# Four-layer image network: the values of the first four units of layer 0 are projected in turns -1 to 2, and the keys' norms are spread at another place

## The chip, the cores and the metric

The kernel runs on one core of a Trainium2 chip. The metric is the device time of one execution in microseconds (us), taken as the median over several runs. An execution covers both images of the batch and all four layers. TensorE does the matrix products (PE in the profile, with its weight loads shown as PEld), VectorE (DVE) and ScalarE (ACT) do most element-wise work, GpSimd (POOL) some of it, and the queue of SyncE (SP) issues the transfers.

## The reference

The input is two images of 512 channels and 64 x 64 pixels in float32. Four residual layers follow each other; each one normalizes its input by groups of channels (16 channels share a mean and a variance), computes something and adds it to its input. The change touches layer 0 alone, so only that is shown, shortened:

```python
q = xf @ W_q + b_q                      # 8 heads of 64 channels, 4096 tokens
q_norm = q / |q|;  q_scaled = (q_norm + query_embedding) * softplus(temperature)
k_l, v_l = xf @ W_kv + b_kv             # k_l is divided by its norm, per head
attn_local = q_scaled . k_l at the 3 x 3 neighbours of each token      # 9 numbers
xs = layernorm(mean over 4 x 4 of gelu(xf @ W_sr + b_sr))              # 256 pooled tokens
k_pool, v_pool = xs @ W_kv + b_kv
attn = softmax(concat(attn_local, q_scaled @ normalized(k_pool)))
lt = q_norm @ learnable_tokens + learnable_bias + attn[:9]
out = (sum over the 9 neighbours of lt * v_l + attn[9:] @ v_pool) @ W_proj + b_proj
```

Layers 1 to 3 (a deformable attention, a mixture of max-pools, and an attention by random features) are the same before and after.

## The kernel before, in words

**Layout.** An image lies in SBUF as four blocks of 128 channels by 4096 tokens. One block of channels is two heads. Layer 0 works on *units*: a unit is one block of channels times 1024 tokens (16 rows of the image), so there are 4 units to a block (`UN`) and 16 in all, taken block after block. Products are made in *blocks* of 512 tokens, one PSUM bank each. A float32 product of 128 x 128 by 512 shows as two instructions, so the projection of one block of tokens (four products over the input channels, line 134, `project`) is eight instructions. Five banks named `mm` serve everything (`bank`), besides one for the sums of the taps and one for a copy of the queries.

**The run of layer 0** (`Local.run`). First the pooled tokens: 32 projections with the gelu. Then a loop over *turns* i = -4 to 16. In turn i the keys of unit i+4 are projected, the queries of unit i+3, and the products of queries with the nine shifted keys (the *taps*) are made for unit i+1; unit i attends to the pooled tokens, and unit i-1 weighs its values by the nine taps. Each of these stages is a Python generator; `in_turn` advances all of them by one step after another, and so ten *rounds* make a turn. The order in which the generators write instructions is the program order. Within a round it is: norms, tap products, attention, weighing, tap sums, projections, spread of the norms (`normed`). A planner (a list scheduler with its own cost model) then orders each engine's instructions by program order as far as it believes them ready. In turns with the flag `steady`, PE alone is excepted: it keeps the program order (`manual_schedule` for PE). Before, `steady` holds in turns 3 to 11.

**Values.** Values are projected by `value`: eight instructions on PE, and an ACTIVATE on ACT (line 2364) that adds the bias and writes the block into the framed image `vx`. When a unit is the last of its block of channels, the next block's weights are fetched by a transfer on SP's queue (`fetch`). In turns 3 and later the values of unit i+1 are made; the values of the first four units are made earlier, unit 0 in turn -4, units 1 and 2 in turn -3, unit 3 in turn -2. Turns -4 to -2 also hold the computation of the pooled keys and values (`pooled_heads`, a chain of small steps over all engines), of which turn -4 has the first twelve steps.

**Norms.** `norms` (round 1 and 2 of a turn) takes the squares of the turn before: products on PE that sum them by heads (line 2303), then on DVE a transpose, an inverse square root by integer shift and three Newton steps, and a transpose back into `sq` (lines 2306 to 2318). `normed` spreads the results over the 64 channels of each head by a small product on PE (line 2330, two for keys and two for queries) and multiplies keys or queries by them on DVE (line 2338). Keys go into the framed image `kx`, queries stay. `learned` then makes the products with the learnable tokens and the scaled queries. In a steady turn the keys' spread stands at the end of round 3, the queries' at the end of round 4, `learned` in round 6; in other turns in rounds 5, 6 and 7.

**Attention and weighing.** `attend` takes four pairs of products with the pooled keys (line 2433, `exponentials`), each followed by exponentials on ACT (line 2437), two groups of products with the pooled values (line 2443, `values(0)` and `values(1)`), and the sum of the exponentials (lines 2459 and 2462). `weigh` reads the spread tap weights back by transfers, copies them into banks on ACT (line 2526), and multiplies them with `vx` on DVE (line 2534); POOL adds (line 2539). In steady turns tap products are made in pairs (five instructions of DVE on line 2381 instead of nine), the third pair is queued behind the last multiplication of the keys, and two half sums of POOL (line 2452) go to `sq`.

Of the kernel before, what the change touches and what calls it, by code (L numbers as in the profile page):

```python
# [12 lines left out]
ALU = mybir.AluOpType  # L13
# [3 lines left out]
P = 128  # L17
C = 512
KC = C // P
W = 64  # L20
# [1720 lines left out]
class Queries:  # L1741
# [29 lines left out]
    def run(self, Y, dst, fp, pp, ppo, ppd, load):  # L1771

        nc, ratio = self.nc, fp.tile([P, NH], F32, name="ksum_ratio")
        self.Y = Y
        nc.vector.reciprocal(ratio, self.ksum[:, 0, :])
        nc.vector.tensor_tensor(ratio, ratio, self.ksum[:, 1, :], ALU.mult)
        in_turn(self.score(0, fp, pp), self.prepare(1, pp))
        for blk in range(NB):
            stages = [self.attend(blk, ratio, dst, fp, pp, ppo, ppd)]
            if 1 <= blk < NB - 1:  # L1780
                stages.append(self.prepare(blk + 1, pp))
            if blk + 1 < NB:
                stages.append(chain([None], self.score(blk + 1, fp, pp)))
            if load and 0 <= blk - 3 < KC:
                stages.append(load(blk - 3))
            if load and 0 <= blk - 4 < KC:
                st = fp.tile([P, NB, 6], F32, name="gn_st0")
                stages.append(self.statistics(Y, st, blk - 4, pp))
            in_turn(*stages)
        big = LIMIT * math.exp(-LIMIT)  # L1790
        nc.vector.reciprocal(self.low, self.low)
        for t in (self.low, self.high):
            nc.vector.tensor_scalar(t, t, big, None, ALU.mult)
            self.net.at_most(t)
# [143 lines left out]
class Local:  # L1938
# [77 lines left out]
    def run(self):  # L2016


        self.nmean = self.net.stats[:, 0]
        xs = self.pooled_tokens()  # L2020
        heads = self.pooled_heads(xs)
        units = KC * self.UN
        unit = lambda u: u if 0 <= u < units else None
        self.pending = []
        for i in "qkv":
            self.fetch(i, 0)
        for i in range(-4, units + 1):
            k, q, ahead, u, before = (unit(i + n) for n in (4, 3, 1, 0, -1))
            self.steady = self.UN <= i + 1 and i < units - 4
            streams, ended = [], []  # L2030
            stages = [self.norms(streams, ended)]
            if ahead is not None:
                stages.append(self.tap_products(ahead))
            if u is not None:
                stages.append(self.attend(u))
            if before is not None:
                stages.append(self.weigh(before))
            if ahead is not None:
                stages.append(self.tap_sums(ahead))
            values = ([ahead] if i >= self.UN - 1 and ahead is not None  # L2040
                      else {-4: [0], -3: [1, 2], -2: [3]}.get(i, []))
            stages.append(self.projections(k, q, values, streams))
            stages.append(self.normed(ended))
            if i < -2:
                stages.append(islice(heads, 12 if i == -4 else None))
            if i == units - 3:
                stages.append(self.fetch_output())
            if i > units - 3:
                stages.append(self.output(i - units + 2))
            if self.steady:  # L2050
                with self.net.tc.manual_schedule(engines={mybir.EngineType.PE}):
                    in_turn(*stages)
            else:
                in_turn(*stages)

        self.nc.sync.dma_start(self.next_w, self.d["w_q1"].rearrange("(kc p) o -> p kc o", p=P))
        in_turn(self.output(KC - 1))
# [263 lines left out]

    def normed(self, ended):

        nc = self.nc
        for _ in range(3 if self.steady else 5):
            yield
        for which in "kq":
            mine = [(e, self.bank()) for e in ended if e[2] == which]
            for (s, rows, *_), ps in mine:
                nc.tensor.matmul(ps, self.cst[32 * s:32 * s + 2, C_ROW:C_ROW + P], rows, start=True,  # L2330
                                 stop=True)
            for (_, _, _, u, j, part, _), ps in mine:
                out = part
                if which == "k":
                    y = 1 + u % self.UN * self.UY + j * self.UY // 2
                    out = self.kx[:, y:y + self.UY // 2, 1:W + 1]
                    part, ps = (a.rearrange("p (y x) -> p y x", x=W) for a in (part, ps))
                self.multiplied = nc.vector.tensor_tensor(out, part, ps, ALU.mult).ins  # L2338
            yield
        if self.steady:  # L2340
            yield
        if mine:
            self.learned(mine[-1][0][3])
        yield

    def learned(self, u):

# [69 lines left out]
        self.el[u] = el  # L2417
        yield

    def attend(self, u):  # L2420

        nc = self.nc
        cc = u // self.UN
        qs, el = self.qs[u % 3], self.el[u]
        out = self.att()
        prob, half = {}, {}
        self.out[u] = out
        heads = [slice(h * HD, (h + 1) * HD) for h in range(2)]

        def exponentials(j, k2):  # L2430
            pS = [self.bank() for _ in range(2)]
            for h, c in enumerate(heads):
                nc.tensor.matmul(pS[h], self.kp[c, cc, k2 * P:(k2 + 1) * P],
                                 qs[c, j * TB:(j + 1) * TB], start=True, stop=True)
            prob[j, k2] = [self.prob() for _ in range(2)]
            for h in range(2):
                nc.scalar.activation(prob[j, k2][h], pS[h], AF.Exp)  # L2437

        def values(j):
            psO = self.bank()  # L2440
            for k2 in range(2):
                for h, c in enumerate(heads):
                    nc.tensor.matmul(psO[c, :], self.vp[:, k2, cc * P + h * HD:][:, :HD],
                                     prob[j, k2][h], start=(k2 == 0), stop=(k2 == 1))
            nc.scalar.copy(out[:, j * TB:(j + 1) * TB], psO)
            halved(j)

        def halved(j):
            if j not in half:
                half[j] = self.halves if not j else self.sq[2:] if self.steady else prob[1, 1]  # L2450
                for h in range(2):
                    nc.gpsimd.tensor_tensor(half[j][h], prob[j, 0][h], prob[j, 1][h], ALU.add)  # L2452

        def sums():
            psD = self.bank()
            blocks = [slice(j * HD, (j + 1) * HD) for j in range(2)]
            for h in range(2):
                for j, b in enumerate(blocks):
                    nc.tensor.matmul(psD[b, :], self.cst[:, C_EVEN + h:C_EVEN + h + HD],
                                     half[j][h], start=(h == 0), stop=False)  # L2460
            for b in blocks:
                nc.tensor.matmul(psD[b, :], self.cst[b, C_SD:C_SD + HD], el[b, :], start=False,
                                 stop=True)
            return psD

        exponentials(0, 0)
        yield
        exponentials(0, 1)
        yield
        if self.steady:  # L2470
            yield
        values(0)
        if not self.steady:
            yield
        exponentials(1, 0)
        yield
        exponentials(1, 1)
        if self.steady:
            halved(1)
        yield  # L2480
        values(1)
        yield
        if not self.steady:
            yield
        psD = sums()

        nc.vector.transpose(psD, psD)
        two = psD.rearrange("p (b n r) -> p b n r", n=16, r=2)[:, :, 0]
        nc.vector.reciprocal(two, two)
        nc.vector.transpose(self.recip.rearrange("p (b n r) -> p b n r", n=16, r=2),  # L2490
                            bcast(two, 2, 16))
        yield
        el = self.el.pop(u)
        nc.vector.tensor_tensor(el, el, self.recip, ALU.mult)
        nc.vector.tensor_tensor(el, el, self.lt.pop(u), ALU.add)
        if self.steady:
            yield
        self.spread = self.rows()
        for j in range(2):
            nc.sync.dma_start(self.spread[:, j * TB:(j + 1) * TB], el[j * HD:(j + 1) * HD, :])  # L2500
        self.fetch_tap(u, 0)
        yield
        self.fetch_tap(u, 1)
        yield
# [231 lines left out]
```

## Time and profile before

| | us |
|---|---|
| runs | 5098.28, 5098.58, 5102.41 |
| median | 5098.58 |
| the profiled execution, its own time | 5100.09 |
| its span, first to last instruction | 5098.3 |
| PE busy in the span | 4835.1 |
| DVE busy | 3067.0 |
| ACT busy | 1817.9 |
| POOL busy | 1843.8 |
| mean granted clock of TensorE | 0.981 |

A turn is best found in the trace by its products on line 2303, of which each turn from -3 on has one group. Counted from there, the turns of the first image begin at 194.16 (turn -3), 230.32 (-2), 253.49 (-1), 285.79 (0), 321.51 (1), 365.32 (2), 411.09 (3), 456.53 (4) and then every 42.54 us. Those of the second image begin at 2726.34, 2760.81, 2785.67, 2817.97, 2853.69, 2897.95, 2943.87 and 2989.63 us. The stretch before turn -3, with turn -4, begins at 153.67 us in the first image and at 2684.60 in the second, where the first products of values are seen.

In a table of stretches each row gives its bounds and its length, for every engine the busy time and the number of instructions, then the granted clock of TensorE (1.00 is full speed), and the transfers' share and rate. In a timeline each row gives start, duration, engine, line, operation, names, shapes and count, and in brackets the idle time of the engine ahead of it and what ended that. Profile names are those of the buffers that the tiles lie in: `vx`, `kx`, keys and queries show as `big`, most small tiles of the layer as `late`.

### The profile page before, as it was taken

How to read it: one execution, taken by the hardware profiler on the slowest of the kernel's cores; microseconds unless marked ns; L12 is line 12 of the kernel's file. 1: busy time of each engine (PE TensorE's matmuls, PEld its weight loads, DVE VectorE, ACT ScalarE, POOL GpSimd, SP SyncE). 2: the span in 40 equal slices, each digit the busy share in tenths (PEclk: the TensorE clock that was granted, in tenths of full speed). 3: DMA queues.
4: the chain of work that ended last, by engine and by line, in shares of the span. 5: the costliest groups of instructions: out<-in, count | busy, mean ns of one | idle time of the engine just before them, and what ended most of it. 6: DMA issues, size and time to landing. Idle time of an engine off the chain costs nothing. (4 is left out here: it accounts for less than half of the span.)

```text
span 5098.3 us, 48031 instructions
## 1 busy us (share of the span) xinstructions
PE 4835.1 (95%) x17027; PEld 1992.3 (39%) x17027; DVE 3067.0 (60%) x4014; ACT 1817.9 (36%) x3479; POOL 1843.8 (36%) x1214
## 2 busy tenths in 40 slices
PE   7999999899999999999999999998999999999998
PEld 3423332555334444433344233335543344444333
DVE  4266777644679533477732677776446794334766
ACT  1245555334323233322112555552343232333221
POOL 0035666500320045454500456654013201454554
PEclk9999999999999999999999999999999999999999
DMA  3035556600000000211110355565000000000111
GB/s 151 3 80 141 149 147 172 169 23 10 1 1 17 2 1 1 67 58 46 56 72 3 95 141 149 147 181 149 19 10 1 17 1 1 1 1 23 38 46 45
DMA packets 124748, 309.82 MB, mean 61 GB/s; under 512 B 20882, under 2 KB 33682, under 8 KB 122964
## 3 DMA queue, kind: packets, MB, share of 16 engines
q1 hardware_dynamic: 124500, 306.68, 20.7%
q8 instruction: 136, 2.23, 0.2%
q14 instruction: 112, 0.92, 0.1%
HBM read 258.11 MB, written 48.50 MB: 60 GB/s over the span
## 5 line engine op out<-in xcount | busy, mean ns | idle before, releaser
L134 PE MATMUL mm<-big,w 128*128 128x512 f32 x2496 | 1178.8, 616 | 33.0 <-DVE big L2338 9.5
L134 PEld LDWEIGHTS mm<-big,w 128*128 128x128 f32 x2496 | 458.0, 193 | 717.8 <-issue 560.1
L2539 POOL TENSOR_TENSOR late<-late,big 128x1024 f32<-128x1024 f32 x192 | 455.4, 2372 | 235.6 <-DVE big L2534 203.5
L2381 DVE TENSOR_TENSOR prods<-qs,big 128x1024 f32<-128x1024 f32 (+1 forms) x216 | 335.3, 1569 | 66.4 <-PE tap L2408 56.2
L1639 POOL TENSOR_TENSOR big<-big 128x512 f32<-128x512 f32 x224 | 277.9, 1274 | 219.3 <-ACT big L1630 219.3
L2534 DVE TENSOR_TENSOR big<-big,mm 128x512 f32<-128x512 f32 x384 | 252.0, 680 | 127.1 <-ACT mm L2526 126.8
L2526 ACT COPY mm<-big 128x512 f32<-128x512 f32 x428 | 245.2, 596 | 124.6 <-DMA big<-rows 80.9
L1630 ACT ACTIVATE big<-mm,ed 128x256 f32<-128x256 f32 x512 | 193.5, 489 | 233.0 <-DVE top L1626 200.4
L2452 POOL TENSOR_TENSOR late<-late 128x512 f32<-128x512 f32 x92 | 115.4, 1274 | 440.3 <-ACT late L2437 416.7
L2539 POOL TENSOR_TENSOR late<-late,tap 128x1024 f32<-128x1024 f32 x96 | 226.7, 2361 | 113.8 <-DVE tap L2534 100.7
L1442 POOL TENSOR_TENSOR wq<-prob 128x512 f32<-128x512 f32 x48 | 70.8, 1497 | 503.1 <-ACT prob L1439 503.1
L1894 PE MATMUL mm<-k,w 128*128 128x512 f32 x512 | 238.5, 609 | 12.5 <-DVE k L1887 7.5
L1626 DVE TENSOR_REDUCE top<-mm 128x1 f32<-128x512 f32 x256 | 158.9, 682 | 148.2 <-PE mm L1557 148.2
L1604 PE MATMUL mm<-w,big 128*128 128x512 f32 x512 | 236.6, 606 | 0.0
L134 PE MATMUL mm<-big,wq 128*128 128x512 f32 x512 | 232.2, 602 | 2.7 <-ACT off_t L1223 2.7
L1195 PE MATMUL mm<-big,wo 128*128 128x512 f32 x512 | 234.7, 604 | 0.0
L1352 PE MATMUL acc<-big,diag 128*128 128x512 f32 x512 | 226.9, 601 | 4.6 <-ACT diag L1357 4.6
L973 POOL TENSOR_TENSOR group_stats<-group_stats,cst 128x1 f32<-128x1 f32 (+1 forms) x20 | 12.1, 622 | 570.6 <-DVE group_stats L972 510.4
L1884 DVE RECIPROCAL psD<-psD 128x512 f32<-128x512 f32 x64 | 215.1, 3361 | 1.9
L134 PE MATMUL mm<-big,big 128*128 128x512 f32 x464 | 201.7, 594 | 0.5 <-DVE b_sr L1011 0.5
L2408 PE MATMUL tap<-prods,cst 128*32 128x512 f32 x1152 | 195.3, 604 | 5.1 <-DVE prods L2381 4.3
L1439 ACT ACTIVATE prob<-mm 128x512 f32<-128x512 f32 x256 | 133.0, 603 | 171.4 <-PE mm L1436 171.1
(404 smaller groups left out, 8154.3 us busy)
## 6 DMA issues: line engine op xcount, KB each, us to landing
big<-rows SPq DMA_DIRECT2D x428, 256.0 KB, 4.1
tap<-rows SPq DMA_DIRECT2D x212, 256.0 KB, 4.1
yd<-late SPq DMA_DIRECT2D x32, 512.0 KB, 3.1
lost_all<-lost SPq DMA_DIRECT2D x128, 128.0 KB, 3.0
out<-big SPq DMA_DIRECT2D x64, 256.0 KB, 2.0
big<-in_W_kv SPq DMA_DIRECT2D x8, 1024.0 KB, 8.7
rows<-late SPq DMA_DIRECT2D x64, 128.0 KB, 3.3
prods<-yd SPq DMA_DIRECT2D x16, 512.0 KB, 4.9
```

The source lines that it names most:

```text
L134: self.nc.tensor.matmul(ps, w[:, kc, :], X[:, kc, blk * TB:(blk + 1) * TB], start=(kc == 0), stop=(kc == KC - 1))
L1195: nc.tensor.matmul(ps, w[:, kc, oc * P:(oc + 1) * P], att[:, kc, :], start=(kc == 0), stop=(kc == KC - 1))
L1352: nc.tensor.matmul(accs[b], dg, src[:, b * TB:(b + 1) * TB], start=(j == 0), stop=(j == 6))
L1604: nc.tensor.matmul(ps, X[:, kc, lo:lo + P], wv[:, kc, :], start=(kc == 0), stop=(kc == KC - 1))
L1639: nc.gpsimd.tensor_tensor(a, a, part, ALU.add)
L1884: nc.vector.reciprocal(psD, psD)
L1894: nc.tensor.matmul(ps, self.wo[:, kc, oc * P:(oc + 1) * P], qs[:, kc, :], start=(kc == 0), stop=(kc == KC - 1))
L2381: self.nc.vector.tensor_tensor(self.pair(u, k)[:, :n].rearrange("p k (y x) -> p k y x", x=W), bcast(qs.rearrange("p (y x) -> p y x", x=W), ...
L2408: nc.tensor.matmul(ps[32 * q:32 * q + 32, :], self.cst[:, C_TAPW + 16 - 2 * k:][:, :32], self.pair(u, k)[:, 0, j * TB:(j + 1) * TB], start ...
L2526: nc.scalar.copy(ps, part)
L2534: nc.vector.tensor_tensor(part.rearrange("p (y x) -> p y x", x=W), self.vx[:, y:y + self.UY // 2, dx:dx + W], ps.rearrange("p (y x) -> p y ...
L2539: nc.gpsimd.tensor_tensor(out, out, t, ALU.add)
```

## The change

The values of unit i+1 are now made in turn i for every i from -1 on; turns -4 to -2 make none. The flag `steady`, with its fixed order on PE, its pairs of tap products and its places of steps, holds in turns 0 to 11. The spread of the keys' norms leaves `normed` in steady turns: it is now called by `attend`, in round 3, behind `values(0)` and ahead of `exponentials(1, 0)`. The spread of the queries' norms stays in round 4, `learned` in round 6.

```diff
         for i in range(-4, units + 1):
             k, q, ahead, u, before = (unit(i + n) for n in (4, 3, 1, 0, -1))
-            self.steady = self.UN <= i + 1 and i < units - 4
+            self.steady = 0 <= i < units - 4
...
             if u is not None:
-                stages.append(self.attend(u))
+                stages.append(self.attend(u, ended))
...
-            values = ([ahead] if i >= self.UN - 1 and ahead is not None
-                      else {-4: [0], -3: [1, 2], -2: [3]}.get(i, []))
+            values = [ahead] if ahead is not None else []
             stages.append(self.projections(k, q, values, streams))
...
     def normed(self, ended):
 
-        nc = self.nc
-        for _ in range(3 if self.steady else 5):
+        for _ in range(4 if self.steady else 5):
             yield
         for which in "kq":
-            mine = [(e, self.bank()) for e in ended if e[2] == which]
...
-            yield
+            if not self.steady or which == "q":
+                last = self.spread_norms(ended, which)
+            if not self.steady:
+                yield
         if self.steady:
             yield
-        if mine:
-            self.learned(mine[-1][0][3])
-        yield
+            yield
+        if last is not None:
+            self.learned(last)
+        yield
+
+    def spread_norms(self, ended, which):
+
+        nc = self.nc
+        mine = [(e, self.bank()) for e in ended if e[2] == which]
+        for (s, rows, *_), ps in mine:
+            nc.tensor.matmul(ps, self.cst[32 * s:32 * s + 2, C_ROW:C_ROW + P], rows, start=True,
+                             stop=True)
+        for (_, _, _, u, j, part, _), ps in mine:
+            out = part
+            if which == "k":
+                y = 1 + u % self.UN * self.UY + j * self.UY // 2
+                out = self.kx[:, y:y + self.UY // 2, 1:W + 1]
+                part, ps = (a.rearrange("p (y x) -> p y x", x=W) for a in (part, ps))
+            self.multiplied = nc.vector.tensor_tensor(out, part, ps, ALU.mult).ins
+        return mine[-1][0][3] if mine else None
...
         if self.steady:
             yield
         values(0)
+        if self.steady:
+            self.spread_norms(ended, "k")
         if not self.steady:
             yield
         exponentials(1, 0)
```

More of the change, by code (lines that the diff above doesn't have):

```diff
@@ L2322, in normed @@
     def normed(self, ended):
-        nc = self.nc
-        for _ in range(3 if self.steady else 5):
+        for _ in range(4 if self.steady else 5):
             yield
         for which in "kq":
-            mine = [(e, self.bank()) for e in ended if e[2] == which]
[L2329 to L2338, printed above, removed]
-            yield
+            if not self.steady or which == "q":
+                last = self.spread_norms(ended, which)
+            if not self.steady:
+                yield
         if self.steady:
             yield
-        if mine:
-            self.learned(mine[-1][0][3])
+            yield
+        if last is not None:
+            self.learned(last)
         yield
+    def spread_norms(self, ended, which):
[12 more added lines that the diff above has]
+        return mine[-1][0][3] if mine else None
     def learned(self, u):
@@ L2418, in tap_sums, with attend @@
         yield
-    def attend(self, u):
+    def attend(self, u, ended):
         nc = self.nc
```

## The prediction

> **What bounds the kernel now.** I read the page first, then a table of stretches over the turns of layer 0, the waits of PE, and the timelines of single turns.
>
> ```profile
> PE 4835.1 (95%) x17027; PEld 1992.3 (39%) x17027; DVE 3067.0 (60%) x4014; ACT 1817.9 (36%) x3479; POOL 1843.8 (36%) x1214
> ```
>
> PE is the bound: a step is worth what it adds to PE's work, its idle time, or its slow clock. The stretches of the first image (turn -4, -3, ... 4):
>
> ```profile
> 153.67:194.16 40.49, 39.38 (x130) 21.18 (x128) 6.42 (x11) 10.06 (x18) 0.71 (x1) 1.00 0.00 1
> 194.16:230.32 36.16, 35.20 (x93) 14.71 (x93) 7.83 (x26) 7.47 (x12) 3.39 (x3) 0.91 0.00 0
> 230.32:253.49 23.17, 22.13 (x66) 8.18 (x65) 11.20 (x23) 8.10 (x12) 0.00 (x0) 1.00 0.04 12
> 253.49:285.79 32.30, 29.65 (x98) 9.30 (x97) 16.34 (x28) 10.82 (x16) 0.00 (x0) 0.95 0.03 9
> 285.79:321.51 35.72, 35.72 (x149) 11.06 (x148) 20.22 (x33) 14.73 (x26) 5.01 (x4) 1.00 0.20 46
> 321.51:365.32 43.81, 40.81 (x149) 12.46 (x146) 32.84 (x55) 24.63 (x44) 26.15 (x13) 0.92 0.47 126
> 365.32:411.09 45.77, 41.80 (x132) 13.49 (x127) 28.91 (x49) 24.66 (x44) 26.08 (x13) 0.93 0.45 126
> 411.09:456.53 45.44, 42.96 (x153) 13.45 (x153) 33.24 (x51) 26.43 (x47) 26.18 (x13) 1.00 0.61 163
> 456.53:499.07 42.54, 41.84 (x153) 13.16 (x153) 32.02 (x49) 25.31 (x45) 26.17 (x13) 1.00 0.55 147
> ```
>
> The point is the rows of turns 1 and 2 (the fourth and third from the end) against the last one. Turns 1 and 2 project no values and yet take 43.81 and 45.77 us; turn 4, with values, takes 42.54. They lose 3.0 and 4.0 us idle and, at clocks of 0.92 and 0.93, 3.5 and 3.2 us of speed. A block of values costs PE 3.43 us (sixteen instructions of line 134 took 7.13, eight 3.70), a unit 6.9. Turn 0, never idle, needs 35.72; with 6.9 added that is turn 4's 42.6. So values in turns 0 to 2 fit, if those turns then run like turn 4.
>
> The lead-in's cover, first in turn -4 (second image), then turns -2 and -1 (first image):
>
> ```profile
> 2688.03 1.89 PE L2109 MATMUL mm<-late,cst 128*128 128x256 f32 x8
> 2689.76 3.60 PE L134 MATMUL mm<-big,w 128*128 128x512 f32 x8
> 2693.19 1.84 PE L2119 MATMUL mm<-cst,late 128*128 128x1 f32 x16
> 2696.12 0.71 PE L2128 MATMUL mm<-cst,ln_rs 128*128 128x128 f32 x4 [1.09 <-POOL ln_rs L2123]
> 2696.67 5.29 PE L134 MATMUL mm<-big,w 128*128 128x512 f32 x8
> ```
> ```profile
> 236.05 1.13 PE L2330 MATMUL mm<-sq,cst 2*128 2x512 f32 x4 [1.04 <-DVE sq L2318]
> ...
> 265.59 1.13 PE L2330 MATMUL mm<-sq,cst 2*128 2x512 f32 x4 [1.73 <-DVE sq L2318]
> ```
>
> The row at 2689.76 is a block of values standing between two links of the pooled chain; the row at 2696.67 is a block of keys that could have filled the 1.09 us ahead of line 2128 and did not. Last, the regular turn on PE, and its DVE one turn later (add 42.54):
>
> ```profile
> 506.00 1.94 PE L2443 MATMUL mm<-late,vp 128*64 128x512 f32 x8
> 507.86 1.13 PE L2433 MATMUL mm<-big,kp 64*128 64x512 f32 x4
> ...
> 509.92 1.13 PE L2330 MATMUL mm<-sq,cst 2*128 2x512 f32 x4
> ...
> 512.63 3.70 PE L134 MATMUL mm<-big,w 128*128 128x512 f32 x8 [0.53 <-DVE big L2338]
> ```
> ```profile
> 548.52 0.72 DVE L2318 STREAM_TRANSPOSE sq<-mm 128x512 f32<-128x512 f32 x1
> 553.84 1.28 DVE L2338 TENSOR_TENSOR big<-big,mm 128x512 f32<-128x512 f32 x2
> ```
>
> Keys are multiplied on DVE at 553.84 to 555.12, and the first block of keys' projection starts then (512.63 + 42.54 = 555.17) after 0.53 us idle: a bank is freed late. The waits of PE put that at 4.7 us for nine turns.
>
> **The change part by part** (for one image; both have the same turns).
>
> *Eight blocks of values leave turns -4 to -2.* 8 x 3.43 = 27.4 us of PE. Their eight evictions on ACT (0.69 us each) are off the path on either side: ACT is busy 8 to 10 us in those turns, 25 of 43 in turns 1 and 2. One transfer of weights (128 x 512 floats, 256 KB) moves on SP's queue from turn -2, where transfers have a share of 0.04, to turn 2, behind the taps' transfers (0.45). It is due at the start of turn 3, some 35 us later; in the regular turns the same transfer leaves no wait on PE. The framing of `vx` on POOL (0.28 and 0.21 us) loses a wait for an eviction.
>
> *The cover that goes.* Six waits of PE's chain stand open without values: last gelu to line 2109 2.7 us (154.1 to 156.83, ACT and three steps of DVE); 2109 to 2119 2.4 (a DVE and an ACT step, 159.46 to 161.77); 2128 to 2145 2.7 (two DVE steps, 166.46 to 169.09), if the keys that now stand there go into the first two; the pooled keys' roots 3.6 (DVE, then 2.90 of POOL, to 199.2); the last eviction of turn -3 1.4; and the norms of turn -2, 4.6 (231.51 to 236.00 on DVE). Sum 17.4. Nothing opens if the planner puts the next projections of keys and queries there, which are owed anyway; all 17.4 if it never does. Both are seen: the 1.09 above was not filled with the keys right behind it, while at 180.62 two instructions of line 2159 went into a wait of line 2152. I take the middle, 8.7.
>
> *Two blocks of values enter turn -1.* 6.9 us, of which its 2.65 us of idle time take the first part: +4.2.
>
> *Slow clock in the lead-in.* It costs 4.9 us now (0.09 x 36.16 + 0.05 x 32.30), in the second image 6.7. Fewer waits in turn -1 and more before speak against each other: 0. Bounds: -5 (none left) and +10 (each of the six waits brings one slow stretch of 3.4 us at half speed, 1.7).
> Here the Trainium skill ("TensorE: Matmul & The Clock Gate", "Why this matters for your kernels") says that waits under about 3 us leave the clock alone. The trace differs: the slow stretch in turn -1 follows a wait of 1.73 us, those of turns 1 and 2 waits of 2.46 and 2.40. By the rule only the waits of 3.6 and 4.6 us could slow it, at most +3.4 in place of +10.
>
> Lead-in: -27.4 + 8.7 + 4.2 + 0 = -14.5; from -28 (no cover lost, no slow clock) to +4 (all open).
>
> *Turns 0 to 3.* Now 35.72 + 43.81 + 45.77 + 45.44 = 170.7 (second image 171.7). After, four regular turns with the keys' spread moved, 4 x 42.01 (below), and half of what turn 3 paid for entering the fixed order (45.44 - 42.54 = 2.9), 1.5, as turn 0 has no weighing: 169.5. That is -1.2 and -2.2. Pairs of tap products save DVE 9 x 1.21 - (4 x 2.28 + 1.21) = 0.6 a turn, off the path. Bounds: -3.7, and +11 if each takes 45.4.
>
> *Keys' spread behind values(0).* No work is added. From line 2303 the regular turn has `values(0)` at +6.9, pooled products at +8.8, the spread at +10.85; DVE has the rows ready at +7.63. The spread goes to +8.8, 1.1 us after its rows, so PE should not wait; DVE is idle from +7.63 to +10.06, multiplies then, and the banks come free near +11.2, ahead of the keys' projection at +13.0. The 0.53 goes. Behind the spread on PE stand the pooled products, which move from +8.8 to +9.85, and their exponentials on ACT; `values(1)`, which needs them, starts at +18.2, so that is covered by 8 us. What is late next is the 0.17 us for an exponential, which stays. In turns 4 to 11: 8 x 0.53 = -4.2. Bounds: -4.2, and +4.2 should the stall come back as large ahead of the second pooled products.
>
> Sum: -14.5 - 1.2 - 4.2 = -19.9 and, in the second image, -20.9; -40.8 in all. From the profiled execution's own 5100.09 us (1.8 more than its span) that makes 5059.3; it stands 1.5 above the median, so the forecast is 5058.
>
> **The rivals.** (a) *The lead-in's waits stay open.* For it: line 2128's unfilled wait. Against it: the planner did fill line 2152's. All of 17.4 and +10 of clock give -27.4 + 17.4 + 4.2 + 10 = +4.2 in the lead-in, less 5.4 elsewhere: -1.2 and, in the second image, -2.2, hence 5095: no difference that can be told. By the page's +3.4 it would be 5082.
>
> (b) *Slower: PE, in fixed order, waits for the norms.* Place: the spread at +8.8 in turns 0 to 11. DVE's chain ends at +7.63 in the regular turns, but at +17.4 in turn 1, +12.3 in turn 2 and +10.66 in turn 3 of before, where weighing and tap products cut in. If the planner orders DVE anew and the chain ends at +10.66 in every such turn, 24 turns wait 1.9 us each, +45; without the spread's gain the rest is worth 2 x -14.5 + 1 = -28. 5098.6 + 45 - 28 = 5116. It decides from about +10.0 (24 x 1.2 = 28) on. Against it: turn 4's DVE, with the same work, ends at +7.63 in both images.
>
> (c) *The spread's move gains nothing*, since DVE still multiplies the keys behind the weighing's products. For it: DVE's order is the planner's. Then 24 x 0.53 = 12.7 are missing: 5071.
>
> **How the numbers follow.** A kernel of this spread can be told from no change from about 0.2% (10 us) on: faster is below 5088, slower above 5109. My forecast (waits half filled, order holds) 0.58; (c) 0.10; (a) 0.18, half of it within 10 us, a third faster, the rest slower by more slow clock; (b) 0.14, nearly all slower. Faster 0.58 + 0.10 + 0.06 = 0.74, of which I give 0.01 away for turns 0 to 2 at 45 us; same 0.09 + 0.01; slower 0.17. The forecast's own range is 5035 to 5080: the lead-in by +/-9 an image, turns 0 to 3 by -2.5 to +3. For 8 in 10 it must take in (c) and most of (a): 5032 (lead-in -27 an image) to 5100, with (b) and the worst of (a) left out.
>
> **What would show it.** Right: turns 0 to 2 at 42 to 43 us from one group of line 2303 to the next at clock 1.00; turns 4 to 11 at about 42.0, with no wait of line 134 for line 2338; the stretch from the first pooled product (157.5) to turn 0 shorter by some 10 us or more, with new waits ahead of lines 2109, 2119 and 2330. Wrong: waits of line 2330 for line 2318 in steady turns (b); turns still at 42.5 (c); a lead-in as long as before with PE idle 17 us more (a); or the planner pulling so much forward that even turn -1 is short, which would bring it under 5032.

## The result: slower by 0.4%

The changed kernel takes 5121.04 us (median of six runs, 5116.47 to 5124.60), the kernel before beside it 5098.68. The ratio is 1.0041, 95% interval 1.0029 to 1.0054. The forecast was 5058, faster; the range ended at 5100. One run of an experiment below, the spread alone, took 6631 us at a mean clock of 0.70, and its ratio leaves it out.

The page of the changed kernel begins so:

```profile
PE 4817.0 (94%) x17027; PEld 1984.3 (39%) x17027; DVE 3063.5 (60%) x3990; ACT 1819.1 (36%) x3479; POOL 1845.1 (36%) x1214
```

PE does the same 17027 instructions, in 18 us less of busy time, over a span 16 us longer. Its idle time grew by 34 us. The stretches of the first image, turn -4, -3, ... 2, then turn 4 (same columns as before: bounds, length, busy times, granted clock, transfers):

```profile
155.23:193.60 38.37, 32.14 (x105) 18.15 (x104) 6.42 (x11) 8.01 (x15) 1.19 (x3) 0.91 0.00 0
193.60:222.93 29.33, 22.26 (x62) 8.90 (x61) 7.16 (x26) 4.17 (x7) 2.91 (x1) 0.77 0.00 1
222.93:253.58 30.65, 25.63 (x66) 9.24 (x65) 11.20 (x23) 9.26 (x14) 0.00 (x0) 0.89 0.00 0
253.58:287.01 33.43, 32.62 (x114) 11.03 (x113) 16.32 (x26) 12.23 (x18) 0.00 (x0) 1.00 0.03 8
287.01:328.71 41.70, 41.70 (x153) 13.17 (x152) 21.18 (x31) 16.23 (x27) 4.99 (x4) 1.00 0.21 53
328.71:372.38 43.67, 41.85 (x154) 13.16 (x153) 31.77 (x49) 25.44 (x45) 26.16 (x13) 1.00 0.47 130
372.38:416.05 43.67, 41.85 (x154) 13.17 (x153) 31.77 (x49) 25.36 (x45) 26.18 (x13) 1.00 0.53 146
...
459.71:503.38 43.67, 41.85 (x154) 13.17 (x153) 31.76 (x49) 25.36 (x45) 26.18 (x13) 1.00 0.53 143
```

Two things are to be seen. Turn 0 starts at 287.01, where it started at 285.79 before, although 17 us of PE work have left the stretch ahead of it (eight blocks of values out, three in: the first block of a turn stands ahead of its group of norms). Of its start 1.4 us are a later end of the pooled products, at 155.66, from which the table below counts. And turns 1 to 10 take 43.67 us, regular at once, but 1.13 above the 42.54 of before; turn 11 takes 44.65, before 43.52. Granted clock is 0.91, 0.77 and 0.89 in the first three rows.

The first image in sums, from the profiled executions, in us. "Lead-in" is from the end of the last pooled product to turn 0's group of norms; "idle" is PE's idle time in it; "slow" is (1 - clock) x length; where PE waits at a slow clock both count, so they overlap. The last four columns are experiments told below.

| us | before | after | values moved, spread old | values early, fixed from 0 | keys in waits | all waits filled |
|---|---|---|---|---|---|---|
| lead-in | 131.5 | 131.4 | 133.4 | 131.5 | 119.8 | 116.5 |
| idle in it | 5.8 | 19.1 | 19.1 | 5.8 | 10.3 | 6.3 |
| slow in it | 5.1 | 13.7 | 17.1 | 5.1 | 8.5 | 6.8 |
| turns 0 to 3 | 170.8 | 172.7 | 169.3 | 157.7 | 169.3 | 166.4 |
| turns 4 to 11 | 341.3 | 350.3 | 341.3 | 341.3 | 341.3 | 340.2 |

So before to after is -0.2 in the lead-in, +1.9 in turns 0 to 3, +9.0 in turns 4 to 11, and -1.3 in turn 12 (44.52 to 43.21): 9.5 in the first image. In the second, counted the same way, it is -0.8, +1.0, +9.0 and +1.2: 10.5. That makes 20 for both; these two executions lie 16.4 us apart, the medians 22.4, and what the other layers add or take was not located. Turn 12 goes either way and is no effect that can be told. Nor are 2 us in a lead-in: up to turn 0 the changed kernel and the first experiment (third column) have the same program and the same idle time, and yet their lead-ins differ by 2.0 (131.4 and 133.4; in the second image 132.4 and 132.3), as their slow clock does (13.7 and 17.1).

The lead-in's balance: eight blocks out (-27.4), three in (+10.3), 13.3 more idle and up to 8.5 more slow clock make at most +4.7; measured is -0.2. Some of the idle time of after lies in slow stretches and counts twice, and in turn -1 the tap products run closer together than before. PE's timeline there:

```profile
158.38 1.97 PE L2108 MATMUL mm<-late,cst 128*128 128x256 f32 x8 [2.72 <-DVE late L2104]
162.74 2.59 PE L2118 MATMUL mm<-cst,late 128*128 128x1 f32 x16 [2.40 <-ACT late L2112]
166.44 1.22 PE L2127 MATMUL mm<-cst,ln_rs 128*128 128x128 f32 x4 [1.11 <-POOL ln_rs L2122]
167.46 5.20 PE L134 MATMUL mm<-big,w 128*128 128x512 f32 x8
...
198.64 0.69 PE L2178 MATMUL mm<-cst,late 128*128 128x128 f32 x2 [3.61 <-POOL late L2172]
...
204.42 2.08 PE L2342 MATMUL mm<-sq,cst 2*128 2x512 f32 x4 [2.45 <-DVE sq L2317]
...
230.05 2.08 PE L2342 MATMUL mm<-sq,cst 2*128 2x512 f32 x4 [4.65 <-DVE sq L2317]
```

Four of the six waits that the prediction listed stand open, in nearly the size reckoned (2.7, 2.4, 3.6, 4.6). The fifth, ahead of line 2144, stays covered by keys, as before; the sixth, for the last eviction of turn -3, is 0.37 instead of 1.4; and one of 2.45, which was not on the list, opens in turn -3. The first block of keys comes at 167.46, after three waits, and runs at the slow clock (5.20 us for eight instructions instead of 3.60). That it could have run earlier is shown by the experiment with the keys in the waits.

A regular turn of the changed kernel, PE, then DVE, then ACT (its group of norms is at 503.38):

```profile
512.17 1.13 PE L2342 MATMUL mm<-sq,cst 2*128 2x512 f32 x4
513.23 1.13 PE L2440 MATMUL mm<-big,kp 64*128 64x512 f32 x4
514.28 1.07 PE L2415 MATMUL tap<-prods,cst 128*32 128x512 f32 x8
515.28 1.13 PE L2440 MATMUL mm<-big,kp 64*128 64x512 f32 x4
518.06 2.41 PE L134 MATMUL mm<-big,w 128*128 128x512 f32 x5 [1.65 <-DVE big L2543]
```
```profile
510.29 0.72 DVE L2317 STREAM_TRANSPOSE sq<-mm 128x512 f32<-128x512 f32 x1
513.33 1.29 DVE L2350 TENSOR_TENSOR big<-big,mm 128x512 f32<-128x512 f32 x2 [2.32 <-PE mm L2342]
514.53 2.29 DVE L2388 TENSOR_TENSOR prods<-qs,big 128x2048 f32<-128x2048 f32 x1
516.73 1.28 DVE L2543 TENSOR_TENSOR big<-big,mm 128x512 f32<-128x512 f32 x2
```
```profile
515.42 0.60 ACT L2535 COPY mm<-big 128x512 f32<-128x512 f32 x1
```

The spread stands at +8.79, its multiplication ends at +11.2 (514.62), as forecast. But the keys' projection (line 134) no longer waits for that multiplication. It waits until 518.01, for a product of the weighing (line 2543; 2534 before). Before, two of the weighing's products stood ahead of the keys' multiplication (at 553.84 in the last lines of the trace in the prediction; that turn's group of norms is at 541.61), and the third pair of tap products behind it:

```profile
551.67 0.69 DVE L2534 TENSOR_TENSOR tap<-big,mm 128x512 f32<-128x512 f32 x1 [2.44 <-ACT mm L2526]
553.23 0.69 DVE L2534 TENSOR_TENSOR tap<-big,mm 128x512 f32<-128x512 f32 x1 [0.87 <-ACT mm L2526]
555.03 2.28 DVE L2381 TENSOR_TENSOR prods<-qs,big 128x2048 f32<-128x2048 f32 x1
```

Now the keys' multiplication comes ahead of the weighing's products, and at its heels the third pair, which is queued behind that multiplication and nothing else: 2.29 us. The weighing's second copy is ready at 516.02 and finds DVE busy.

### The profile page after: what moved, and what is told of

It is laid out like the page before. It is cut to its first block, busy times and chain, and to the rows that moved or that the text cites. A ratio compares the mean times of both kernels' runs of the same rounds, so it can differ in the third digit from the quotient of the medians.

```text
span 5114.7 us, 48015 instructions
## 1 busy us (share of the span) xinstructions
PE 4817.0 (94%) x17027; PEld 1984.3 (39%) x17027; DVE 3063.5 (60%) x3990; ACT 1819.1 (36%) x3479; POOL 1845.1 (36%) x1214
## 5 line engine op out<-in xcount | busy, mean ns | idle before, releaser
L2459 POOL TENSOR_TENSOR late<-late 128x512 f32<-128x512 f32 x80 | 100.5, 1279 | 432.3 <-ACT late L2444 419.8
L1526 POOL TENSOR_TENSOR sq<-k 128x512 f32<-128x512 f32 x128 | 133.3, 1043 | 155.4 <-ACT k L1524 139.1
```

## The experiments

The theory after this reading: the spread's new place costs the regular turns by the order that it brings about on DVE, and the moved values gain nothing because they were the lead-in's cover. The rivals: the fixed order in turns 0 to 2 costs; the late bank has a cause other than DVE's order; the lead-in is bound by its chain whatever PE does. Each run is compared with the kernel before on the same chip, which is given with it.

### Values moved, the spread in its old place

```diff
-        if self.steady:
-            self.spread_norms(ended, "k")
...
-        for _ in range(4 if self.steady else 5):
+        for _ in range(3 if self.steady else 5):
             yield
         for which in "kq":
-            if not self.steady or which == "q":
-                last = self.spread_norms(ended, which)
-            if not self.steady:
-                yield
-        if self.steady:
-            yield
-            yield
+            last = self.spread_norms(ended, which)
+            yield
+        if self.steady:
+            yield
```

> The change without its last part: values moved and order fixed from turn 0, the keys' spread back at the end of round 3. Theory (the spread's new place costs 1.13 us in each of turns 1 to 11, the moved values are worth nothing because the waits of the lead-in open): turns 1 to 11 at 42.5 us, lead-in as in the changed kernel, 22 x 1.13 = 25 us less than the changed kernel's 5121, so 5096. Rival (the fixed order in turns 0 to 2 is what costs): turns 0 to 3 longer than 42.6 and a total above 5105.

Measured: 5095.23 us (before: 5102.31), ratio 0.9984, interval 0.9975 to 0.9994. Its turns 0 to 2:

```profile
287.61:329.32 41.71, 41.71 (x154) 13.17 (x153) 21.18 (x31) 16.22 (x27) 4.99 (x4) 1.00 0.21 55
329.32:371.86 42.54, 41.84 (x154) 13.16 (x153) 32.02 (x49) 25.28 (x45) 26.17 (x13) 1.00 0.46 129
371.86:414.40 42.54, 41.84 (x153) 13.16 (x152) 32.01 (x49) 25.29 (x45) 26.15 (x13) 1.00 0.56 152
```

The fixed order costs nothing: turns 1 and 2 now hold a unit of values and are shorter than before without (43.81 and 45.77). Moving the values and fixing the order gain 0.16% together, as the theory said, and the spread turns that into the loss.

### The spread alone

In the kernel before, `attend` makes the keys' spread as in the change, and `normed` skips it.

```diff
         for which in "kq":
+            if self.steady and which == "k":
+                yield
+                continue
             mine = [(e, self.bank()) for e in ended if e[2] == which]
...
         values(0)
+        if self.steady:
+            self.spread_keys(ended)
```

> The kernel before with the keys' spread behind values(0) in turns 3 to 11 and nothing else. Theory: those turns go from 42.54 to 43.67 us, 18 x 1.13 = 20 us more, 5119, and PE's wait ahead of the keys' projection is for the weighing's product on DVE. Rival (the longer turns come from the values' new place or the earlier start of the fixed order): turns at 42.0 to 42.6 and a total of 5089 to 5099.

Measured: 5125.46 us (before: 5102.31), ratio 1.0042, interval 1.0029 to 1.0056. Turns 4 to 10 take 43.67. For seven regular turns before and six here, the waits of PE (line waited for, total, times, longest):

```profile
PE mm L134 <- DVE big L2338: 3.7, 7, 0.5
PE mm L134 <- ACT late L2437: 1.2, 7, 0.2
```
```profile
PE mm L134 <- DVE big L2552: 6.6, 4, 1.7
PE mm L134 <- DVE tap L2552: 3.3, 2, 1.7
PE mm L134 <- ACT late L2453: 1.0, 6, 0.2
```

The second is over six turns, 9.9 us or 1.65 a turn. The wait for the keys' multiplication, 0.53 a turn, is gone, and one for the weighing's product (line 2552 here) is in its place. The difference, 1.12, accounts for the 1.13 a turn, and this part alone makes the whole loss.

### The third pair behind the weighing's products

As the last run, and the third pair of tap products waits its turn on DVE:

```diff
-            held = (self.net.tc.issue_after(self.multiplied) if self.steady and k == 4
-                    else nullcontext())
-            with held:
+            with ExitStack() as held:
+                if self.steady and k == 4:
+                    held.enter_context(self.net.tc.issue_after(self.multiplied))
+                    if self.weighed:
+                        held.enter_context(self.net.tc.issue_after(self.weighed))
...
-                nc.vector.tensor_tensor(
+                self.weighed = nc.vector.tensor_tensor(
...
```

> The spread alone moved (as in the run before this but one), and on DVE the third pair of tap products queued behind the weighing's products of round 3 as well as behind the keys' multiplication. Theory (the wait is for a bank of the weighing whose product on DVE stands behind the held pair of 2.29 us): the second copy ends at +12.6, its product can end at +13.3, PE waits 0.3 to 0.4 us instead of 1.66: turns of 42.3 to 42.5, total 5094 to 5099. Rival (ACT's copy or the bank itself comes late whatever DVE does): turns stay at 43.3 or more, total 5112 or more.

Measured: 5093.69 us (before: 5102.31), ratio 0.9984, interval 0.9974 to 0.9994. Turns 4 to 10 take 42.40. DVE and PE in a regular turn (group of norms at 499.39):

```profile
509.34 1.29 DVE L2359 TENSOR_TENSOR big<-big,mm 128x512 f32<-128x512 f32 x2 [2.32 <-PE mm L2354]
510.54 0.68 DVE L2554 TENSOR_TENSOR big<-big,mm 128x512 f32<-128x512 f32 x1
512.07 0.69 DVE L2554 TENSOR_TENSOR big<-big,mm 128x512 f32<-128x512 f32 x1 [0.84 <-ACT mm L2546]
512.67 2.28 DVE L2399 TENSOR_TENSOR prods<-qs,big 128x2048 f32<-128x2048 f32 x1
```
```profile
512.81 3.70 PE L134 MATMUL mm<-big,w 128*128 128x512 f32 x8 [0.39 <-DVE big L2554]
```

One instruction, the pair, changed its place on DVE, and 1.26 of the 1.65 us went. What is left, 0.39, is ACT's copy that comes late. So the cause is DVE's order, and the spread's new place is worth 0.14 a turn, not 0.53, once that is mended.

### Values early, the order fixed from turn 0

The kernel before with one line changed:

```diff
-            self.steady = self.UN <= i + 1 and i < units - 4
+            self.steady = 0 <= i < units - 4
```

> The kernel before with the flag steady from turn 0 instead of 3; values stay in turns -4 to -2, the keys' spread stays at the end of round 3. Theory (values are free filler in the lead-in's waits, and turns 1 and 2 were slow by their order alone): lead-in as before, turns 0 to 2 at 35.7 to 36.5 us, turn 3 at 42.5: 171 - 151 = 20 us less per image, 5058. Rival (without values something other than PE bounds a turn, DVE with 32 us or the taps' transfers): turns 1 and 2 at 40 us or more, 5075 to 5095.

Measured: 5072.95 us (before: 5102.31), ratio 0.9937, interval 0.9921 to 0.9954. Turns 0 to 3:

```profile
285.95:320.74 34.79, 34.79 (x138) 10.42 (x136) 18.63 (x29) 14.33 (x25) 5.00 (x4) 1.00 0.18 42
320.74:359.50 38.76, 37.24 (x138) 11.49 (x137) 31.58 (x50) 24.00 (x44) 25.72 (x13) 0.96 0.53 145
359.50:401.10 41.60, 39.78 (x146) 12.33 (x144) 34.46 (x52) 25.67 (x47) 26.67 (x14) 1.00 0.58 165
401.10:443.64 42.54, 41.84 (x153) 13.16 (x152) 32.02 (x49) 25.31 (x45) 26.16 (x13) 1.00 0.55 149
```

The result lies between the two numbers, and each is right in part: the lead-in is as before, and turns 0 to 3 give 13.1 us in the first image and 14.1 in the second, not 20. Turn 1 has 38.76 and turn 2 38.2 without a block of turn 3's values that lies in its stretch (41.60 - 3.43), where 35.7 to 36.5 had been expected. They are idle for 1.5 and 1.8 us, most of it in waits for DVE, and turn 1 has a clock of 0.96. Against the first run, which differs by the place of values alone, it is 22 us faster: in the lead-in values are nearly free; in turn 0 two blocks cost all of their 6.9 us, in turn 1 two cost 3.8, and in turn 2 the one by which the runs differ costs 0.9 of its 3.4.

### The first keys and queries in the lead-in's waits

The first run (values moved, spread old) with two stages written earlier; no work is added:

```diff
         made, taken = ((4, 6, 7, 8), (0, 2)) if self.steady else ((6, 7, 8, 9), (0, 3, 6, 9))
+        if uk == 0:
+            made = (0, 3, 8, 9)
+        elif uq == 0:
+            made = (6, 7, 0, 3)
```

(The queries' squares keep their buffers 2 and 3.)

> The run with values moved and the keys' spread in its old place, with one more edit: in turn -4 the first unit's keys are projected in rounds 0 and 3, and in turn -3 the first unit's queries in rounds 0 and 3, where values stood before; nothing else moves and no work is added. Theory (the planner keeps program order on PE, so a wait is covered only by what is written there): the waits ahead of lines 2108, 2118 and 2178 close (2.7 + 2.4 + 3.6), one of 2.7 opens ahead of line 2144, 6 to 8 us of idle time and 2 to 4 of slow clock less per image: 5071 to 5080, with that run at 5095. Rival (the chain of pooled keys and norms sets the end of the lead-in whatever PE does meanwhile): 5090 to 5096.

Measured: 5066.76 us (before: 5098.77), ratio 0.9931, interval 0.9916 to 0.9947. PE's timeline:

```profile
153.71 3.60 PE L134 MATMUL mm<-big,w 128*128 128x512 f32 x8
157.15 1.89 PE L2108 MATMUL mm<-late,cst 128*128 128x256 f32 x8
158.87 3.60 PE L134 MATMUL mm<-big,w 128*128 128x512 f32 x8
162.31 1.84 PE L2118 MATMUL mm<-cst,late 128*128 128x1 f32 x16
165.25 0.71 PE L2127 MATMUL mm<-cst,ln_rs 128*128 128x128 f32 x4 [1.10 <-POOL ln_rs L2122]
167.80 8.62 PE L2144 MATMUL mm<-late,big 128*128 128x256 f32 x32 [1.83 <-DVE late L2131]
...
191.73 3.60 PE L134 MATMUL mm<-big,w 128*128 128x512 f32 x8
195.50 0.44 PE L2178 MATMUL mm<-cst,late 128*128 128x128 f32 x2 [0.17 <-POOL late L2172]
```

That is less than the 5071 to 5080 expected. Three waits (2.7, 2.4 and 3.6) are closed by blocks that had to be made anyway, the one of 2.45 shrinks to 0.28, and one of 1.83 opens. The lead-in goes from 133.4 to 119.8: 13.6 us, of which 8.8 are idle time; the other 4.8 are slow clock, which fell by 8.6 in all, partly under the same waits. In the second image it goes from 132.3 to 120.8: 11.5, of which 8.8 are idle time again and 2.7 slow clock. So the planner had not filled waits of this length with work written later, though that work could run; the order in the program decides, and rival (a) of the prediction is how the lead-in behaves.

### The change, mended

The changed kernel with the third pair behind the weighing's products (the edit shown above).

> The changed kernel with the one edit that the third pair of tap products is queued on DVE behind the weighing's products of round 3 too. Theory (the changed kernel's loss is the 1.66 us that PE waits for the weighing's bank; the moved values gain little): turns 1 to 11 at 42.4 us in place of 43.67, 22 x 1.27 = 28 us less than the changed kernel, 5093, about 9 below the kernel before. Rival (in turns 1 to 3 another wait takes its place): 5105 or more.

Measured: 5091.84 us (before: 5098.77), ratio 0.9985, interval 0.9976 to 0.9994; turns 1 to 10 at 42.40. All the loss was that order on DVE; what is left of the change's worth is 7 us.

### Units 0 to 2 early, unit 3 in turn 2

The mended change with

```diff
-            values = [ahead] if ahead is not None else []
+            values = ([ahead] if i >= self.UN - 1 and ahead is not None
+                      else {-4: [0], -3: [1], -2: [2], 2: [3]}.get(i, []))
```

> The changed kernel with two edits: the values of units 0, 1 and 2 go back to turns -4, -3 and -2, one unit a turn, those of unit 3 are made in turn 2, and turns -1 to 1 make none; and the third pair of tap products is queued on DVE behind the weighing's products of round 3. Theory (values are worth their 3.43 us a block where PE waits anyway, two blocks for each of the turns -4 to -2; the others cost the same wherever they stand, and turn 2 has some 2 us of idle time for them): against the run of the kernel before with steady from turn 0, lead-in 6.9 us shorter, turn 2 some 4 us longer, regular turns 42.4 in place of 42.54; 2 x (2.9 + 1.7) = 9 us less than 5073, so 5064, with the kernel before at 5102. Rival (waits of turns 1 and 2 come from the first weighing and the values of unit 3 only add): 5070 or more.

Measured: 5070.23 us (before: 5098.77), ratio 0.9941, interval 0.9928 to 0.9955: the rival's number. The lead-in went from 131.5 to 124.8, as reckoned. But turn 1 has no values, and there the spread, which now stands early, meets a chain of norms that is not done:

```profile
323.31 1.13 PE L2343 MATMUL mm<-sq,cst 2*128 2x512 f32 x4 [3.46 <-DVE sq L2318]
```

That is rival (b) in one turn. In the run before this one, turn 1 has the values and no such wait: the block of values of round 2, which stands between the squares' sums and the spread, is what gives DVE the time.

### All waits filled

The mended change, the first keys and queries as in the run with keys in waits, and

```diff
-            values = [ahead] if ahead is not None else []
+            values = ([ahead] if i >= self.UN - 1 and ahead is not None
+                      else {-2: [0], -1: [1], 1: [2], 2: [3]}.get(i, []))
```

> The first unit's keys and queries in the waits of turns -4 and -3 (as in the run with keys in the waits), the keys' spread behind values(0) with the third pair behind the weighing's products, and the values of units 0, 1, 2 and 3 in turns -2, -1, 1 and 2; turn 0 makes none. Theory (a block is free where PE waits or runs slow for it, and costs 3.43 us elsewhere): against the run with keys in the waits, turn -2 takes 6.9 us of values for 5.1 us of idle time and some 3 of slow clock, turn 0 is 6.2 us shorter (35.5 as in the run with units 0 to 2 early), 11 turns at 42.4 in place of 42.54: 2 x (1.5 + 6.2 + 1.5) = 18 us less than 5067, so 5048, with the kernel before near 5099. Rival (a wait in turn 0 or 1 opens without turn 0's values, as in turn 2 of the run with units 0 to 2 early): 5058 or more.

Measured: 5056.98 us (before: 5105.13), ratio 0.9908, interval 0.9891 to 0.9924: the fastest of all, 0.9% below the kernel before, and between the theory's 5048 and the rival's 5058. Turns 0 and 1 took 39.15, with one block of turn 1's values in the stretch, and 42.41; a new wait of 0.67 for the norms opened in turn 0, none in turn 1. Against the run with keys in waits the first image gained 3.3 in the lead-in, 2.9 in turns 0 to 3 and 1.1 in turns 4 to 11, the second 3.7, 3.0 and 1.1: 7.3 and 7.8, where 9.2 were expected. Turn 12 lost 1.3 in the first (41.77 to 43.12) and gained 1.5 in the second (43.38 to 41.92). What is missing, of which the new wait is 0.67, was not followed up.

## Why the prediction was wrong, point by point

**Lead-in, -14.5: wrong.** It measured -0.2. Of that, 3.4 is a slip: the sum took two blocks of values where three lie ahead of turn 0's group of norms. Of the six waits four opened, at the prices reckoned; one stayed covered, one was 0.37 instead of 1.4, and one of 2.45 was overlooked. The choice of the middle, 8.7, failed, and so did "slow clock: 0". Idle time grew by 13.3, slow clock by 8.5 (partly the same time). The profile had the answer in the row that was set against the other: a wait of 1.09 with the keys right behind it, not filled. The counterexample, line 2159 in a wait of line 2152, was work that stood next in the program. Rival (a), given 0.18, is what happened in the lead-in.

**Two blocks in turn -1, +4.2: right in kind.** Its stretch, with two blocks in it, grew from 32.30 to 33.43 us, +1.1 and not +4.2: the slow clock of 0.95 went too, and the tap products, which had stood in groups of four with short waits for DVE, ran closer together (sixteen in 1.92 us, where four had taken 1.05).

**Turns 0 to 3, -1.2: the number nearly right, by two errors.** With the spread in its old place they take 169.3 against 170.8. The 1.5 for entering the fixed order was not paid (turn 0 takes 41.71, the next three 42.54 to 42.55), and the 0.53 a turn was not saved; the two errors nearly cancel. In the changed kernel the spread makes them 172.7.

**Keys' spread, -4.2: wrong, and outside its bounds of +/-4.2.** It measured +9.0 over turns 4 to 11. The place at +8.8, the rows at +7.63 and the multiplication ending near +11.2 were exact. What failed is "the banks come free near +11.2, ahead of the keys' projection at +13.0. The 0.53 goes": the projection's bank is then not the keys' but the weighing's, and "what is late next" was sought on PE alone. The change moves two instructions on DVE as well, and with them the pair that is queued behind them; that pair's 2.28 us, at 555.03, were in the same timeline. That the bank changes hands by the order in which banks are taken is inferred from the releaser that the trace names. That DVE's order decides is shown by the run with the pair behind.

**Rival (b)** did not occur in the changed kernel: DVE's chain ended at +7.63 in turns 1 to 11. It was seen only where a turn had no values. **Rival (c)** had the right part, but neither its mechanism nor its price: the keys were multiplied ahead of the weighing's products, not behind them, and the stall did not stay but grew.

## What to carry to other kernels

Work that looks misplaced because it stands early may be what covers a chain's waits: before it is moved, list those waits, and write something else into each. When an instruction is moved on one engine, follow its consumer on the next engine, and all that is queued behind that consumer by an explicit order; a bank that is handed round can make the next user wait for another reader than before. A stretch that is slow without the work may be fixed by its order alone, which is cheaper to try than to move the work.

## What was not expected of the hardware

The clock cost more than half of what waiting did. In turn -4 of the changed kernel no wait is longer than 2.72 us, yet its granted clock is 0.91: 3.5 us lost, at 6.2 us of idle time. In turn -3, with waits of 3.61 and 2.45, it is 0.77: 6.7 us lost, at 7.1. The Trainium skill ("TensorE: Matmul & The Clock Gate", "Why this matters for your kernels") advises against idle gaps above about 3 us, which the prediction read as leaving shorter ones free; here shorter ones were enough. The kernel before shows it too: turn -1 has a clock of 0.95 with no wait above 1.73 us, and turn -3 one of 0.91 with 0.96 us idle in all and no wait above 0.52. Its slow stretch there follows a row of small products, so the length of waits alone does not tell when the clock drops; what does was not found. When waits of the lead-in were closed, 8.8 us of idle time went in each image and with them 4.8 and 2.7 us of slow clock: for this chain, as an estimate from these two (4.8 / 8.8 and 2.7 / 8.8), 0.3 to 0.5 us of slow clock for each us of waiting.
